# Projecting layer 0 of a graph network by 22 tiles of 128 rows while its neighbour sums stay in 24 blocks of 113

## The chip, the cores and the metric

The kernel runs on one core of a Trainium2 chip. The metric is device microseconds of one execution of the whole program, the median of several runs. The engines are called PE (TensorE, matmuls), DVE (VectorE), ACT (ScalarE), POOL (GpSimd) and SP (SyncE, which here only issues DMAs). Each runs its own instructions in order.

## The reference

Four layers share one sparse adjacency matrix of 2708 x 2708 (about five entries in a row) and node features of 2708 x 512, all float32. After each layer the features are added to the layer's result and normalized over their 512 columns. Only layer 0 and what layer 1 reads from it matter here:

```python
# layer 0
e1 = adj @ x
e2 = e1 * (learnable_diag_1 + 1.0)
x1 = layernorm(x + (x - e2) @ weight + bias)
# what layer 1 reads of x1
h  = x1 @ W_sa                      # 512 columns, and two score columns h @ a_sa
hb = x1 @ W_gcnb                    # 512 columns
# and four gate columns x1 @ Wa, x1 @ Wb (two halves of each)
```

Layer 1 then sums h with attention weights and hb with the adjacency's values over neighbours; layers 2 and 3 aggregate over the same neighbours.

## The kernel before

The adjacency is used as lists. Its rows are cut into 24 blocks of R = 113 rows (`rows(i)`, the last has 109), so that one block's entries fit into 4 chunks of 128. For each block the kernel loads the 113 columns of the transposed adjacency (`load_adj`, three buffers in turn), finds the nonzero entries on DVE, brings them into a list, fetches the neighbours' rows of x from HBM with 4 indirect DMAs on POOL (`gather`), and sums them on PE with a spread matrix as the stationary operand.

The order on every engine is written out by hand, in a prologue and then a loop over `k` from 1 to 23. In step k different blocks are at different stages:

- Block k+3 is searched. `find` runs over four segments of the block's columns, a `max` and a `max_index` each (L831, L833); `count` (from L845) then computes where each entry goes. `negatives` is a 2.3 us pass of ACT over the block, `clear_diagonal` one of POOL.
- Block k+2 becomes a list. `starts` is a tiny matmul (L873), `ranges` its two ACT operations (`middle`, L880, and `q`, L881) and one on DVE (`rec_all`, L882), `mark` a comparison on DVE (L890), `fetch` four matmuls (L895) that need the mark, `pick` ten small DVE operations (L904 to L933) that need the fetch and start the gather, `values0` eight ACT operations that make the spread matrix.
- Block k+1 is summed: `sums0` (l0a on PE, L611), `inputs0` on DVE (L958 to L964: own rows times the diagonal entry, plus sum, times the diagonal weights, plus own rows; the last of the four adds the bias to the own rows `xi` for later), and `turn_u` (tr_l: four transposes on PE and a copy by ACT).
- Block k is projected: `project0` (o_l on PE, L582), `residual0` (L975 on DVE, then ACT), `norm0` (ACT writes the new features to `xr[:, k, :]` in SBUF).
- Block k-1 gets its part of layer 1's table: `turn_x` (tr_x), `next0` (h on PE in two halves of 259 columns, the last six of which are scores and gates and are copied to `cols[:, i, :]`), `rest0` (hb on PE), and `store0` one step later, which sends the rows to `table[0]` in HBM.

The order within a step is what the prediction walks through. On PE it is starts, tr_x, o_l, fetch, h, l0a, hb, tr_l of the next block. On DVE it is rec_all, one search, mark, one search, residual, pick, two searches, count, inputs. `move_rows` splits a row move so that its first part has a multiple of 16 rows. After the loop, layer 1 begins with gathers from `table[0]`, which need every row of it.

Of the kernel before, what the change touches and what calls it, by code (L numbers as in the profile page):

```python
# [12 lines left out]
P = 128  # L13
# [5 lines left out]
R = 113  # L19
# [428 lines left out]
def sparse_stack(  # L448
# [51 lines left out]
    xr = big.tile([P, NB, D], FP, name="xr")  # L500
# [48 lines left out]
    cols = const.tile([P, NB, 6], FP, name="cols")  # L549
# [13 lines left out]
    def move_rows(r, dst, src):  # L563

        c = r // 16 * 16
        for a, b in ((0, c), (c, r)):
            nc.sync.dma_start(out=dst(a, b), in_=src(a, b))

    def turned(u, r, name):

        tr = ps_tr.tile([P, DB, P], FP, tag="tr", name=f"tr_{name}")
        for f in range(DB):
            nc.tensor.transpose(tr[:, f, :r], u[:r, f * P : (f + 1) * P], ident[:r, :r])  # L573
        uT = work.tile([P, DB, P], FP, tag="uT", name=f"uT_{name}", bufs=3)
        nc.scalar.copy(uT[:, :, :r], tr[:, :, :r])  # L575
        return uT
# [65 lines left out]
    with ExitStack() as phase:  # L642
# [41 lines left out]
        def load_own(i):  # L684
            r = rows(i)
            xi = work.tile([P, D], FP, tag="xi", name=f"xi{i}", bufs=3)
# [6 lines left out]
        )  # L693
        gath0 = [
            gflat[k // 2][:, k % 2 * EC * D :][:, : EC * D].rearrange("p (c d) -> p c d", d=D)
            for k in range(4)
        ]
        nc.scalar.memzero(gflat[0])
# [90 lines left out]
        def turn_w(k):  # L789
# [3 lines left out]
            wT = work.tile([P, DB, P], FP, tag="uT", name=f"w_saT{k}", bufs=3)  # L793
# [81 lines left out]
        def ranges(i):  # L875

            t = made[i]
            q = lst.tile([P, EC * P], FP, tag="q", name=f"q{i}")
# [21 lines left out]
        def pick(i):  # L900
# [28 lines left out]
            gather(gath0[i % 4], i, x, D)  # L929
# [21 lines left out]
        def sums0(i):  # L951
            agg0[i] = aggregate(spread0.pop(i), gath0[i % 4], rows(i), f"l0a{i}")

        def inputs0(i):
# [9 lines left out]
            nc.vector.tensor_add(xi[:r, :], xi[:r, :], b0_bc[:r, :])  # L964
            u0[i] = u

        def project0(i):
            o0[i] = project(turned0.pop(i), rows(i), w0_sb, f"l0_{i}")

        def residual0(i):  # L970

            r = rows(i)
            v = work.tile([P, D], FP, tag="v", name=f"l0v{i}")
            stats = small.tile([P, 5], FP, tag="stats0", name=f"st_l0_{i}")
            nc.vector.scalar_tensor_tensor(  # L975
                v[:r, :], o0.pop(i)[:r, :], 0.0, own.pop(i)[:r, :], op0=ALU.add, op1=ALU.add,
# [10 lines left out]
            v0[i] = v, stats  # L987

        def norm0(i):
            r = rows(i)  # L990
            v, stats = v0.pop(i)
# [3 lines left out]
                xr[:r, i, :], v[:r, :], AF.Identity, bias=stats[:r, 4:5], scale=stats[:r, 3:4]  # L995
            )

        def next0(i):

            r = rows(i)  # L1000
            xT = turned0["x", i]
            st = st_ring[i % 2]
            half = (D + 6) // 2
            ends = (0, half, D)
            for k in range(2):
                o = ps_o.tile([P, D], FP, tag="o", name=f"h{k}_{i}")
# [5 lines left out]
            nc.scalar.copy(cols[:r, i, :], col)  # L1012
            nc.scalar.copy(st[:r, 2 * D + 1 : 2 * D + 4], col[:, 1:4])
            st0[i] = st

        def rest0(i, between=lambda: None):
            xT = turned0.pop(("x", i))
            o = ps_o.tile([P, D], FP, tag="o", name=f"hb_{i}")
            times(o[: rows(i), :], xT, rows(i), w_gc_sb, between)
            st0[i] = st0[i], o  # L1020

        def store0(i):
            r = rows(i)
            st, o = st0.pop(i)
            nc.scalar.copy(st[:r, D + 1 : 2 * D + 1], o[:r, :])
            move_rows(
                r, lambda a, b: table[0][i * R + a : i * R + b, :], lambda a, b: st[a:b, :]
            )

        def turn_u(i):  # L1030
            turned0[i] = turned(u0.pop(i), rows(i), f"l0_{i}")

        def turn_x(i):
            turned0["x", i] = turned(xr[:, i, :], rows(i), f"x1_{i}")
# [94 lines left out]

        project0(0)  # L1130
        find(3, (0,), places=False)
        starts(2)
        ranges(2)
        gate_columns()
        turn_w(0)
        mark(2)
        fetch(2)
        find(3, (0,), values=False)
        residual0(0)
        turn_w(1)  # L1140
        pick(2)
        own[2] = load_own(2)
        sums0(1)
        times_a(0)
        turn_w(2)
        norm0(0)
        inputs0(1)
        times_a(1)
        turn_w(3)
        turn_u(1)  # L1150
        values0(2)
        times_a(2)
        times_a(3)
        score_rows()
        find(3, (1, 2, 3))
        clear_diagonal(4)
        count(3)
        negatives(3)
        load_adj(6)
# [6 lines left out]
        for k in range(1, NB):  # L1166
            m, b = k + 2, k + 3
            if k == 1:
                turn_x(k - 1)
                project0(k)  # L1170
            if m < NB:
                starts(m)
                if k == 1:
                    score_columns()
                ranges(m)
            if k > 1:
                turn_x(k - 1)
                project0(k)
                store0(k - 2)
            if b < NB:  # L1180
                negatives(b)
                find(b, (0,))
            if m < NB:
                mark(m)
                if k > 1:
                    fetch(m)
            if b < NB:
                find(b, (1,))
            residual0(k)
            if b + 1 < NB:  # L1190
                clear_diagonal(b + 1)
            if k == 1:
                next0(k - 1)
                fetch(m)
            if m < NB:
                pick(m)
                own[m] = load_own(m)
            norm0(k)
            if k > 1:
                next0(k - 1)  # L1200
            if m < NB:
                values0(m)
            if b < NB:
                find(b, (2, 3))
# [581 lines left out]
```

## Time and profile before

| | |
|---|---|
| median of 3 runs | 1010.57 us (1010.06 to 1011.61) |
| profiled execution | 996.16 us, of which the span is 994.3 us |
| PE, DVE, ACT, POOL busy in the span | 92%, 71%, 53%, 48% |
| mean granted PE clock | 0.97 |
| one step of the loop in its steady part | 15.95 us |
| last matmul of layer 0 (hb of block 23) ends | 427.8 us into the span |
| first gather of layer 1 | 432.95 us |
| DMA share, 100 to 375 us | 0.38 to 0.75 |

The engines' busy times overlap. PE's busy time is a model of pipelined matmuls; the distance from one group's start to the next's is the better measure of what a group takes, and the prediction uses that. A float32 matmul over 4 slices of 128 shows as 8 records.

### The profile page before, as it was taken

The page shows a single profiled execution, that of the slowest core. Times are in us where ns is not written, and L with a number is a line of the kernel's source. Part 1 is how long each engine was busy: PE and PEld are TensorE (multiplying, and loading weights), DVE is VectorE, ACT ScalarE, POOL GpSimd, SP SyncE. Part 2 cuts the span into 40 slices and gives each one's busy share as a digit, 9 for nine tenths or more (in the row PEclk, how much of TensorE's full clock was granted, in tenths as well). Part 3 has the DMA queues.
Part 4 walks back from the last instruction along what each step waited for, and adds up shares of the span by engine and source line. Part 5 has one row for each costly group of instructions (what it writes and reads, how often), then busy time and mean ns, then how long its engine had stood idle before and what let it go on. Part 6 is the DMA issues. An engine that isn't in the chain of part 4 may idle for free. (4 is left out here: it accounts for less than half of the span.)

```text
span 994.3 us, 11251 instructions
## 1 busy us (share of the span) xinstructions
PE 913.7 (92%) x3037; PEld 496.8 (50%) x3037; DVE 709.1 (71%) x1956; ACT 528.3 (53%) x1174; POOL 480.1 (48%) x543
## 2 busy tenths in 40 slices
PE   7889999999999999988888888889988989999994
PEld 3445555555555555546666666633333334444441
DVE  7788888888888883238888878858777615555543
ACT  5676676766667674346767767415455412322222
POOL 3232323323132322045666666467777568776640
PEclk8899999999999999989999999979999999999998
DMA  9965757575665533368999999346777656555531
GB/s 248 286 157 163 198 154 204 160 205 162 191 185 160 152 106 104 94 200 271 315 304 306 312 301 295 122 142 201 219 210 228 176 149 180 169 169 162 167 109 31
DMA packets 126715, 190.55 MB, mean 192 GB/s; under 512 B 81065, under 2 KB 81111, under 8 KB 126643
## 3 DMA queue, kind: packets, MB, share of 16 engines
q0 software_dynamic: 36864, 111.73, 38.4%
q1 hardware_dynamic: 89779, 78.02, 27.5%
q8 instruction: 26, 0.43, 0.2%
q14 instruction: 46, 0.38, 0.1%
HBM read 176.28 MB, written 27.80 MB: 205 GB/s over the span
## 5 line engine op out<-in xcount | busy, mean ns | idle before, releaser
L598 POOL DMA_INDIRECT gath<-table,source x288 | 314.9, 1093 | 139.7 <-issue 66.7
L598 POOL DMA_INDIRECT gath<-in_x_dram,source x96 | 96.7, 1007 | 261.3 <-issue 222.7
L1347 PE MATMUL l1s<-gath,s 128*113 128x256 f32 (+3 forms) x384 | 94.6, 401 | 26.8 <-DVE l1b L1377 26.6
L611 PE MATMUL l2a<-gath,s_left 128*113 128x512 f32 (+1 forms) x192 | 96.5, 623 | 13.0 <-DMA gath<-table,source 10.2
L575 ACT COPY uT_l<-tr_l 128x452 f32<-128x452 f32 (+1 forms) x48 | 25.9, 540 | 138.2 <-PE tr_l L573 138.2
L1347 PEld LDWEIGHTS l1s<-gath,s 128*113 128x113 f32 (+1 forms) x384 | 68.9, 184 | 52.9 <-DVE l1b L1377 34.8
L582 PE MATMUL o_l<-w_sb,uT_l 128*113 128x512 f32 (+1 forms) x192 | 91.8, 623 | 2.2 <-ACT uT_l L575 1.1
L611 PE MATMUL l3a<-gath,s 128*113 128x512 f32 (+1 forms) x192 | 88.5, 603 | 3.5 <-DMA gath<-table,source 3.5
L582 PE MATMUL h<-w_sa_sb,uT_x 128*113 128x259 f32 (+1 forms) x384 | 88.3, 382 | 0.8 <-ACT w_sa_sb L815 0.8
L1357 PE MATMUL l1e<-gath,e 128*113 128x257 f32 (+3 forms) x384 | 87.1, 379 | 0.4 <-DVE e L1340 0.4
L582 PE MATMUL o_l<-shared,uT_l 128*113 128x512 f32 (+1 forms) x192 | 86.5, 593 | 0.6 <-ACT uT_l L575 0.6
L611 PE MATMUL l0a<-gath,s 128*113 128x512 f32 (+1 forms) x192 | 87.1, 596 | 0.0
L582 PE MATMUL hb<-w_gc_sb,uT_x 128*113 128x512 f32 (+1 forms) x192 | 86.6, 593 | 0.0
L1357 PEld LDWEIGHTS l1e<-gath,e 128*113 128x113 f32 (+1 forms) x384 | 68.0, 177 | 15.9 <-DVE e L1340 0.8
L582 PEld LDWEIGHTS h<-w_sa_sb,uT_x 128*113 128x113 f32 (+1 forms) x384 | 66.1, 177 | 16.1 <-issue 1.0
L1705 ACT ACTIVATE y<-l3v,mv_l 113x512 f32<-113x512 f32 (+1 forms) x24 | 19.5, 813 | 88.0 <-DVE mv_l L1701 83.5
L611 PEld LDWEIGHTS l2a<-gath,s_left 128*113 128x113 f32 (+1 forms) x192 | 30.6, 182 | 68.6 <-DMA gath<-table,source 40.7
L582 PEld LDWEIGHTS o_l<-shared,uT_l 128*113 128x113 f32 (+1 forms) x192 | 33.9, 178 | 48.8 <-issue 47.0
L582 PEld LDWEIGHTS hb<-w_gc_sb,uT_x 128*113 128x113 f32 (+1 forms) x192 | 33.9, 178 | 46.5 <-issue 41.5
L582 PEld LDWEIGHTS o_l<-w_sb,uT_l 128*113 128x113 f32 (+1 forms) x192 | 33.2, 183 | 45.6 <-issue 38.5
L611 PEld LDWEIGHTS l3a<-gath,s 128*113 128x113 f32 (+1 forms) x192 | 32.4, 180 | 42.3 <-issue 39.1
L611 PEld LDWEIGHTS l0a<-gath,s 128*113 128x113 f32 (+1 forms) x192 | 34.2, 179 | 38.4 <-issue 36.7
(244 smaller groups left out, 1644.8 us busy)
## 6 DMA issues: line engine op xcount, KB each, us to landing
shared<-in_adj_dram SPq DMA_DIRECT2D x14, 1186.5 KB
table<-st SPq DMA_DIRECT2D x23, 450.2 KB
shared<-table SPq DMA_DIRECT2D x23, 448.0 KB
gath<-in_adj_dram SPq DMA_DIRECT2D x7, 1186.5 KB
xi<-in_x_dram SPq DMA_DIRECT2D x23, 224.0 KB
table<-xr SPq DMA_DIRECT2D x23, 224.0 KB
table<-y SPq DMA_DIRECT2D x23, 224.0 KB
out_dram<-y SPq DMA_DIRECT2D x23, 224.0 KB
```

Source lines behind the costliest of these rows:

```text
L575: nc.scalar.copy(uT[:, :, :r], tr[:, :, :r])
L582: nc.tensor.matmul(o, lhsT=uT[:, f, :r], rhs=w[:, f, :], start=(f == 0), stop=(f == DB - 1))
L598: nc.gpsimd.indirect_dma_start(out=g[:, c, :n], out_offset=None, in_=src[:, :], in_offset=bass.IndirectOffsetOnAxis(ap=source[:, i, c : c ...
L611: nc.tensor.matmul(agg[:r, :], lhsT=s[:, c, :r], rhs=g[:, c, off : off + D], start=(c == 0), stop=(c == EC - 1),)
L1347: nc.tensor.matmul(sum_s[i][:r, k, : at.stop - at.start], lhsT=s[:, c, :r], rhs=g[:, c, at], start=(c == 0), stop=(c == EC - 1),)
L1357: nc.tensor.matmul(sum_e[i][:r, k, k : k + at.stop - at.start], lhsT=e[:, c, :r], rhs=g[:, c, at], start=(c == 0), stop=(c == EC - 1),)
L1705: nc.scalar.activation(y[:r, :], v[:r, :], AF.Identity, bias=mv[:r, 3:4], scale=mv[:r, 2:3])
```

## The change

The sums, lists and searches stay in blocks of 113 rows. The projections, the norm, and layer 1's table are now computed by 22 windows of 128 rows (the last has 20). `turn_u` still transposes a block at a time, but ACT copies its columns into the one or two windows that they belong to (`uw`, three buffers). A window is projected in the first step in which all its rows are there, one window a step at most: `window_at` maps steps to windows, and steps 8 and 17 have none. Its own rows of x are loaded once more (`load_window`), and `bias0` adds the bias to those. The new features are written to `x1w`, in window order, and `to_blocks` moves them and the six score and gate columns by DMA to the block order of `xr`, whose rows become 518 wide and hold `cols` at their end.

The search is taken out of the steps: `search(n)` does the next n segments wherever they belong. A step does four; in steps 3, 4, 5, 12, 13, 14 it does five, in steps 9 and 18 (after a step without a window) one. Projection 0 moves from the prologue into the loop, which now has 26 steps, from 0. The windows' buffers take half of a gather buffer, so there are three gather buffers for four, and two of `uT` and `xi` for three. `load_diagonal` and two tiny loads move ahead of the loop.

```diff
-    xr = big.tile([P, NB, D], FP, name="xr")
+    xr_cols = big.tile([P, NB, D + 6], FP, name="xr")
+    xr = xr_cols[:, :, :D]
...
+        def load_window(w):
+            move_rows(
+                wrows(w), lambda a, b: xw[w % 2][a:b, :],
+                lambda a, b: x[w * P + a : w * P + b, :],
+            )
+
+        def to_blocks(w):
+
+            g, end = w * P, w * P + wrows(w)
+            while g < end:
+                i, q = g // R, g % R
+                n = min(end, (i + 1) * R) - g
+                move_rows(
+                    n, lambda a, b: xr_cols[q + a : q + b, i, :],
+                    lambda a, b: x1w[w % 2][g - w * P + a : g - w * P + b, :],
+                )
+                g += n
...
-            nc.vector.tensor_add(xi[:r, :], xi[:r, :], b0_bc[:r, :])
+            own.pop(i)
             u0[i] = u
+        def bias0(w):
+            r = wrows(w)
+            nc.vector.tensor_add(xw[w % 2][:r, :], xw[w % 2][:r, :], b0_bc[:r, :])
...
         def turn_u(i):
-            turned0[i] = turned(u0.pop(i), rows(i), f"l0_{i}")
+            u, r = u0.pop(i), rows(i)
+            tr = ps_tr.tile([P, DB, P], FP, tag="tr", name=f"tr_l0_{i}")
+            for f in range(DB):
+                nc.tensor.transpose(tr[:, f, :r], u[:r, f * P : (f + 1) * P], ident[:r, :r])
+            a = i * R
+            while a < i * R + r:
+                w = a // P
+                b = min(i * R + r, (w + 1) * P)
...
+                nc.scalar.copy(
+                    window_uT[w][:, :, a - w * P : b - w * P], tr[:, :, a - i * R : b - i * R]
+                )
+                a = b
...
+        window_at, step = {}, 0
+        for w in range(KB):
+            step = max(step + 1, (min(w * P + P, N) - 1) // R)
+            window_at[step] = w
+        to_find = [(b, g) for b in range(3, NB) for g in range(NG)]
+        def search(n):
+            for _ in range(min(n, len(to_find))):
+                b, g = to_find.pop(0)
+                if g == 0:
+                    negatives(b)
+                find(b, (g,))
+                if g == 1 and b + 1 < NB:
+                    clear_diagonal(b + 1)
+                if g == NG - 1:
+                    count(b)
+                    if b + NA < NB:
+                        load_adj(b + NA)
...
+        for k in range(NB + 2):
+            m = k + 2
+            w, wx = window_at.get(k), window_at.get(k - 1)
+            parts = 4
+            if any(t not in window_at for t in (k + 3, k + 4, k + 5)) and 2 < k < NB - 6:
+                parts = 5
+            if k > 2 and wx is None:
+                parts = 1
             if m < NB:
                 starts(m)
...
                 ranges(m)
+            if wx is not None and k <= NB:
+                turn_x(wx)
+            if w is not None:
+                project0(w)
+            if k - 2 in window_at:
+                store0(window_at[k - 2])
+            search(1)
             if m < NB:
                 mark(m)
+                fetch(m)
...
+            if parts > 1:
+                search(1)
+            if w is not None:
+                residual0(w)
             if m < NB:
                 pick(m)
                 own[m] = load_own(m)
+            if k + 1 in window_at:
+                load_window(window_at[k + 1])
+            if w is not None:
+                norm0(w)
+            if wx is not None:
+                next0(wx)
             if m < NB:
                 values0(m)
+            search(parts - 2)
             if k + 1 < NB:
                 sums0(k + 1)
                 inputs0(k + 1)
+            if k + 1 in window_at:
+                bias0(window_at[k + 1])
...
+            if wx is not None:
+                rest0(wx, (lambda: turn_x(w)) if k == NB else (lambda: None))
             if k + 1 < NB:
                 turn_u(k + 1)
...
```

## The prediction

> **What bounds the kernel now.** I first read the table of 25 us windows: for each, the busy time of TensorE (PE), its weight loads, VectorE (DVE), ScalarE (ACT) and GpSimd (POOL), then PE's granted clock, the DMA share and GB/s.
>
> ```profile
> core 0: us, PE busy (x) PEld busy (x) DVE busy (x) ACT busy (x) POOL busy (x), PEclk, DMA share, GB/s
> 50.00:75.00 25.00, 21.84 (x84) 11.51 (x83) 21.85 (x64) 19.58 (x45) 7.31 (x9) 0.98 0.65 157
> 250.00:275.00 25.00, 24.89 (x99) 14.86 (x98) 21.53 (x64) 17.75 (x40) 5.68 (x6) 1.00 0.61 172
> 400.00:425.00 25.00, 24.77 (x89) 13.76 (x89) 6.57 (x20) 7.84 (x26) 0.00 (x0) 1.00 0.25 70
> ```
>
> From about 72 us to 428 us, the end of layer 0, PE never rests, DVE has about a seventh of its time free, DMA a third. Before 72 us PE does wait. The chain of waits only covers layer 3, which is untouched, so layer 0 has to be read from PE's timeline. One steady step (start, duration, instructions; in brackets an idle time before it and what ended it):
>
> ```profile
> 249.58 0.55 PE L573 MATMUL tr_l<-ident,l0u 113*128 113x113 f32 x4
> 249.97 0.29 PE L873 MATMUL fetched<-totals,under 128*128 128x1 f32 x2
> 250.12 0.58 PE L573 MATMUL tr_x<-ident,xr 113*128 113x113 f32 x4
> 250.76 3.69 PE L582 MATMUL o_l<-w_sb,uT_l 128*113 128x512 f32 x8
> 254.29 1.03 PE L895 MATMUL fetched<-rec_all,q 128*128 128x96 f32 x8
> 255.15 3.68 PE L582 MATMUL h<-w_sa_sb,uT_x 128*113 128x259 f32 x16
> ```
>
> After it come l0a (258.66) and hb, each 3.43 long, and the next tr_l at 265.53: a step is 15.95 us. Start to start, o_l takes 3.53, the fetch 0.86, h 3.51. The same step on DVE:
>
> ```profile
> 246.34 0.75 DVE L958 SCALAR_TENSOR_TENSOR l0u<-xi,adiag,l0a 113x512 f32<-113x512 f32 x1 [0.32 <-PE l0a L611]
> 247.85 0.69 DVE L963 TENSOR_TENSOR l0u<-l0u,xi 113x512 f32<-113x512 f32 x1
> ...
> 250.80 0.19 DVE L882 SCALAR_TENSOR_TENSOR rec_all<-fetched,far 128x32 f32<-128x32 f32 x1 [1.53 <-ACT middle L880]
> 252.65 0.47 DVE L890 TENSOR_SCALAR q<-q,totals 128x512 f32<-128x512 f32 x1
> ```
>
> DVE's first work of a step, rec_all, starts 1.22 us after tr_l and its last that PE needs, L963, ends at 248.6, 1.0 us before tr_l. With the 0.32 us wait for l0a, **DVE's slack is only 1.3 us a step**. The mark (L890) releases PE's fetch, with 1.2 us to spare now.
>
> Last, what PE's idle times cost:
>
> ```profile
> 72.37 0.58 PE L573 MATMUL tr_l<-ident,l0u 113*128 113x113 f32 x4 [2.27 <-DVE l0u L963]
> ...
> 73.58 5.39 PE L582 MATMUL o_l<-w_sb,uT_l 128*113 128x512 f32 x8
> ...
> 452.28 5.43 PE L1347 MATMUL l1s<-gath,s 128*113 128x256 f32 x16 [3.01 <-DVE l1b L1377]
> 484.88 3.74 PE L1347 MATMUL l1s<-gath,s 128*113 128x256 f32 x16 [1.95 <-DVE l1b L1377]
> 577.99 5.43 PE L1347 MATMUL l1s<-gath,s 128*113 128x256 f32 x16 [1.93 <-DVE l1b L1377]
> ```
>
> Idles of 1.93, 2.27 and 3.01 us were followed by half clock and 1.7 us lost; one of 1.95 was not.
>
> **What the Trainium skill says.** "TensorE: Matmul & The Clock Gate", section "Back-to-back issue gap", has the spacing depend on the columns streamed, not on the rows kept. The trace agrees: hb of the last block, 109 rows, takes 3.43 us as with 113. Section "What's actually happening" gates the clock after an idle window of about 3.4 us; here idles near 2 us already did it in part of the cases, so I use the trace. Section "Step-by-step: what each phase is for" says matmuls stay in program order, only weight loads move ahead: so a fetch that waits holds h behind it. "DMA: Bandwidth & Descriptors", "Issuing engines are not separate DMA queues": all queues share 16 engines; the added moves must fit into the 0.61 share.
>
> **The change, part by part** (reference 996.2 us, the profiled execution, of which the span is 994.3; the runs' median is 1010.57, 1.4% more, so I add the difference to that).
>
> *Two projections fewer.* 22 windows for 24 blocks removes two each of o_l, h and hb, some 21 us of PE in all. Where they go decides. In step k, o_l is of window w and h, hb of the window of step k-1. A window needs the block holding its last row, so w stands at step (128w+127)//113: 1 to 7, not 8, then 9 to 16, not 17, 18 to 23; the last, of 20 rows, at 24. Counted from step 2 (72.37 us), the new loop drops o_l in steps 8 and 17 and tr_x, h, hb in 9 and 18, but adds step 24 and moves everything one step later. Net: one o_l, h, hb and tr_x: 3.53 + 3.51 + 3.43 + 0.39 = **-10.9 us**. The other set leaves the head.
>
> *Head.* Until 72.37 DVE ends last (tr_l waited 2.27 us for it). It loses block 0's residual (0.75), one 0.69 us add that now follows the inputs, and about 2 us of waits: for ACT's middle behind the 2.3 us negatives (1.59 at 58.7 us) and for PE's o_l of block 0. It keeps all 8 searches and the wait for the Sqrt chain. The window load that bias0 waits for is queued behind two adjacency blocks, which stop loading DMA at 46 us, and the diagonal loads (4.0 us of SP): landed by about 52, needed at 53. I take **-3.3** (bounds -5 to 0, as PE will be cold there).
>
> *Full steps.* 17 stay. turn_u now copies in two pieces. A 452-element ACT copy takes 0.54, one of 6 elements 0.17, so about 0.17 fixed: both pieces 0.70. o_l needs only the first, so it starts some 0.1 us earlier: **-1.7**; middle and rec_all come 0.18 later, within DVE's slack. A transpose of 128 rows adds 0.05, counted. Other edits cost nothing: the bias add moved behind the inputs that PE waits for; two uT, two xi and three gather buffers suffice, since each is last read a step before it is refilled; a gather is issued over 5.2 us, from 8 us into a step, and read 15 us later.
>
> *Five searches in steps 3, 4, 5, 12, 13, 14* (one in 9 and 18). A search is 1.5 to 1.75 us of DVE; 1.0 of slack at L963, less than 0.1 at l0a after the 0.18: tr_l is late by about 0.65. Six times: **+3.9**. Afterwards each list's last search and count() (1.3 us) stand ahead of mark, in steps 6 to 9 and 15 to 18. Fetch comes 0.15 late in the full ones: **+0.6**.
>
> *The gap steps.* In step 8 there is no o_l to cover mark. From tr_l: rec_all 1.22, search from 1.33 to 2.83, count and hand-over 1.31, mark 0.47, so fetch at 4.65; PE is idle from 0.97, **3.7 us, as long as the o_l it dropped**. Then fetch 0.86, h 3.51, l0a 3.43, hb 3.43: 15.9, the old step again. Step 9: mark ends at 4.7, fetch until 5.6, l0a until 9.05; no hb covers DVE's three input operations (2.3), so tr_l waits 2.4: 11.5. Step 10's first copy is 0.2 late behind values0. Together 27.6 where 2 x 15.95 - 0.2 - 10.9 = 20.8 would be free of waits: +6.75, twice: **+13.5**.
>
> *Clock.* Idles of 3.7 us in steps 8 and 17: 1.7 each; those of 2.4 before 10 and 19, half of the time: **+5.1** (0 to 8).
>
> *Moves.* Per window SP gains one load of 256 KB and up to four SBUF copies (265 KB), each priced near the 0.3 us that a row move takes now: under 2 us of SP's 16, where it is about 5 busy. Their bytes are about 2 us of DMA at the 310 GB/s of the step's full stretches, while some 3.5 us of a step are idle. norm0 waits for the copies of two steps earlier. No later work is queued behind them but the next adjacency load, two steps early. I take 0, up to +10, if window loads land after bias0 and hold DVE; none below zero, as they only add work.
>
> *End of layer 0.* Layer 1's first gather waits for the last table rows: ACT copy done at 428.6, gather at 432.95. 20 rows instead of 109: **-1.1** (0 to -2). cols now arrive by DMA, a price the trace lacks for SBUF to SBUF; at about 3 us as for that table store they land before the exp table is loaded (429.9). xr's wider row changes no element count: 0.
>
> Sum: -10.9 - 3.3 - 1.7 + 3.9 + 0.6 + 13.5 + 5.1 - 1.1 = **+6.1 us**: 1002.3 profiled, 1016.7 as median.
>
> **Rivals.** (1) *The cover works*: 21 us of PE really vanish, if ACT and DVE enter a gap step ahead of PE. For it: DVE has 14% free and the three searches done early shorten step 9. Against: rec_all hangs on tr_l, which PE itself issues, so DVE can't be ahead. With gap losses of 4 instead of 13.5 and no cold clock: -8.5, 1002 us; it decides where the two pairs lose less than about 12 us in all, clock included. (2) *They cancel*: the clock stays up and the head gains 5: about -0.7, 1009.9. (3) *DMA or SP becomes the bound*: window load behind an adjacency load in steps 6, 7, 15, 16, where that now comes early: +6 on top, 1023. (4) The change not doing what it says: 22 PE groups are in its instruction order, so no.
>
> **Numbers.** My forecast 0.58, rival 1 0.16, rival 2 0.12, rival 3 0.14. 0.2%, 2 us, is about what can be told from no change. Faster 0.16, same 0.12, slower 0.72. The range, 1004 to 1025, leaves out most of rival 1 and takes in a clock loss of 8 and part of the moves' bound.
>
> **What would show it.** Steps of 15.85 us; 16.5 where five searches run; PE idle of about 3.7 us ahead of fetch in steps 8 and 17 with h slow behind it, and 2.4 us ahead of tr_l a step later; hb of the last window ending near 435 us, from 427.8; layers 1 to 3 as long as now. Gap pairs of 21 to 23 us would prove me wrong, and so would DVE waiting for a DMA at bias0.

## The result and the profile after

| | before | after | ratio, 95% interval |
|---|---|---|---|
| median, first comparison | 1010.06 us (5 runs) | 1019.53 us (1016.02 to 1020.60, 5 runs) | 1.0089 (1.0067 to 1.0110) |
| median, second comparison | 1009.23 us | 1020.61 us | 1.0138 (1.0104 to 1.0171) |
| layer 0 ends in the profile (last hb) | 427.8 us | 437.8 us; 440.3 in a second profile | |
| span of the profiled execution | 994.3 us | 1016.9 us; 1014.7 | |

The change makes the kernel slower by 0.9% to 1.4%, 9.5 us in the first comparison, where 6.1 was forecast. The profiled spans lie 22.6 us apart. Of this 10.0 are layer 0; the other 12.6 are not the change's, as the first experiment shows. Each set of runs below came from one chip, and the time after layer 0 goes with the chip and not with the kernel: 565 to 567 us in the four profiles from chip 4 and in the first profile of the kernel before, 574 to 583 in the eight from chips 2, 13 and 15 and in the first profile after (on which chips the two first profiles ran is not known). The medians differ in the same way (the kernel before has 993 us on chip 4, 1009 to 1012 on the others), so only ratios within one set are compared. Layer 0's end is read as the start of the matmul that follows the last hb.

First the table of 25 us windows of the changed kernel, with the columns as before: the span's stretch, its length, busy times of PE, PEld, DVE, ACT and POOL, then PE's granted clock, DMA share and GB/s.

```profile
core 0: us, PE busy (x) PEld busy (x) DVE busy (x) ACT busy (x) POOL busy (x), PEclk, DMA share, GB/s
50.00:75.00 25.00, 19.74 (x67) 9.48 (x66) 20.48 (x60) 16.07 (x34) 7.59 (x9) 0.90 0.82 219
250.00:275.00 25.00, 24.52 (x92) 14.96 (x92) 23.11 (x74) 14.43 (x36) 4.62 (x6) 1.00 0.82 225
400.00:425.00 25.00, 24.89 (x81) 12.70 (x80) 7.54 (x21) 7.84 (x25) 0.00 (x0) 1.00 0.46 139
```

In the middle line, a stretch with five searches in a step, DVE is now busy 23.1 of 25 us, from 21.5, and the DMA share is 0.82, from 0.61: little of DVE's slack is left there. PE still works 24.5 of the 25 us.

PE's timeline of the changed kernel shows where it rests. A step is counted from one tr_l to the next. In order: the start of step 2, the start of step 5 behind a five-search step, steps 8 and 9 and the start of 10, a steady step (11), and the start of step 19.

```profile
70.71 0.99 PE L1071 MATMUL tr_l<-ident,l0u 113*128 113x113 f32 x4 [4.99 <-DVE l0u L991]
...
122.79 0.58 PE L1071 MATMUL tr_l<-ident,l0u 113*128 113x113 f32 x4 [0.50 <-DVE l0u L991]
...
171.35 0.55 PE L1071 MATMUL tr_l<-ident,l0u 113*128 113x113 f32 x4
...
176.03 2.02 PE L923 MATMUL fetched<-rec_all,q 128*128 128x96 f32 x8 [3.50 <-DVE q L918]
177.85 4.48 PE L584 MATMUL h<-w_sa_sb,uT_x 128*128 128x259 f32 x16
182.16 3.60 PE L613 MATMUL l0a<-gath,s 128*113 128x512 f32 x8
185.60 3.60 PE L584 MATMUL hb<-w_gc_sb,uT_x 128*128 128x512 f32 x8
189.03 0.55 PE L1071 MATMUL tr_l<-ident,l0u 113*128 113x113 f32 x4
...
200.74 0.58 PE L1071 MATMUL tr_l<-ident,l0u 113*128 113x113 f32 x4 [2.39 <-DVE l0u L991]
...
216.56 0.55 PE L1071 MATMUL tr_l<-ident,l0u 113*128 113x113 f32 x4
...
217.57 3.61 PE L584 MATMUL o_l<-w_sb,uw 128*128 128x512 f32 x8
...
343.21 0.94 PE L1071 MATMUL tr_l<-ident,l0u 113*128 113x113 f32 x4 [2.38 <-DVE l0u L991]
```

Step 8 runs from 171.35 to 189.03, 17.68 us: the fetch waits 3.50 us for the mark (L918), takes 2.02 us where 1.03 is its usual time, and h 4.48 for 3.69: half clock through the fetch and into h. Step 9 is 11.71 us long and ends in 2.39 us of idle. The steady step ends at 232.28, so it is 15.72 us. tr_l in step 19 takes 0.94 us, half clock again after an idle of 2.38; the same idle ahead of step 10 left the clock up (0.58).

DVE's timeline in step 8 gives the reason for the 3.50 us. The lines are the first work of the step, its first search (two lines), and the mark; left out are the search's load line and the nine operations of `count`.

```profile
172.57 0.19 DVE L910 SCALAR_TENSOR_TENSOR rec_all<-fetched,far 128x32 f32<-128x32 f32 x1 [2.25 <-ACT middle L908]
172.68 0.74 DVE L859 MAX8 rec_all<-shared 128x8 f32<-128x565 f32 x1
...
173.53 0.74 DVE L861 FIND_INDEX8 where_all<-rec_all,shared 128x8 uint32<-128x565 f32 x1
...
175.50 0.48 DVE L918 TENSOR_SCALAR q<-q,totals 128x512 f32<-128x512 f32 x1
```

DVE waits 2.25 us for ACT's middle, which hangs on tr_l of PE; then 1.5 us of search and 1.3 us of count go ahead of the mark, and with no o_l on PE nothing runs beside them.

### The profile page after: what moved, and what is told of

Its sections match the earlier page's. It is cut to its first block, busy times and chain, and to the rows that moved or that the text cites. A ratio compares the mean times of both kernels' runs of the same rounds, so it can differ in the third digit from the quotient of the medians.

```text
span 1016.9 us, 11285 instructions
## 1 busy us (share of the span) xinstructions
PE 905.9 (89%) x2965; PEld 502.1 (49%) x2965; DVE 703.7 (69%) x1948; ACT 522.0 (51%) x1171; POOL 475.2 (47%) x543
## 4 chain that ended last, share of the span: by engine, by line
PE 59%; DVE 19%; DMA 8%; issue 5%; POOL 3%; ACT 2%; another core or an unknown queue 2%; SPq 0%; POOLq 0%; DVEq 0%; ACTq 0%
PE o_l L584 12%; PE l2a L613 9%; PE l3a L613 8%; DMA gath<-table,source 7%; PE l0a L613 6%; PE h L584 6%; PE hb L584 5%; PE unread L1523 4%; DVE where_all L861 3%; DVE rec_all L859 3%; POOL gath L600 2%; PE fetched L923 2%; PE tr_l L1071 1%; PE tr_l L575 1%
## 5 line engine op out<-in xcount | busy, mean ns | idle before, releaser
L613 PE MATMUL l2a<-gath,s_left 128*113 128x512 f32 (+1 forms) x192 | 94.1, 634 | 2.1 <-DVE s_left L1560 2.0
L613 PE MATMUL l0a<-gath,s 128*113 128x512 f32 (+1 forms) x192 | 89.9, 613 | 0.0
L584 PE MATMUL o_l<-w_sb,uw 128*128 128x512 f32 (+1 forms) x176 | 83.5, 618 | 0.7 <-ACT uw L1080 0.4
L584 PE MATMUL h<-w_sa_sb,uT_x 128*128 128x259 f32 (+1 forms) x352 | 83.6, 391 | 0.0
L584 PE MATMUL hb<-w_gc_sb,uT_x 128*128 128x512 f32 (+1 forms) x176 | 79.5, 593 | 0.0
L584 PEld LDWEIGHTS h<-w_sa_sb,uT_x 128*128 128x128 f32 (+1 forms) x352 | 65.5, 191 | 12.8 <-issue 1.8
L1523 PE MATMUL unread<-bg_bc,ident 128*128 128x512 f32 x88 | 47.6, 662 | 20.6 <-remote 16.3
L613 PEld LDWEIGHTS l2a<-gath,s_left 128*113 128x113 f32 (+1 forms) x192 | 34.9, 192 | 52.5 <-issue 47.1
L1732 DVE SCALAR_TENSOR_TENSOR l3v<-o_l,d_inv,b_bc 113x512 f32<-113x512 f32 (+1 forms) x25 | 18.1, 729 | 55.4 <-PE o_l L584 50.5
L584 PEld LDWEIGHTS hb<-w_gc_sb,uT_x 128*128 128x128 f32 (+1 forms) x176 | 32.5, 186 | 40.9 <-issue 39.5
```

The costliest lines, as they stand in the source:

```text
L584: nc.tensor.matmul(o, lhsT=uT[:, f, :r], rhs=w[:, f, :], start=(f == 0), stop=(f == DB - 1))
L613: nc.tensor.matmul(agg[:r, :], lhsT=s[:, c, :r], rhs=g[:, c, off : off + D], start=(c == 0), stop=(c == EC - 1),)
L1523: nc.tensor.matmul(o[:, :cols], lhsT=ident, rhs=bg_bc[:, :cols], start=True, stop=True)
L1732: nc.vector.scalar_tensor_tensor(v[:r, at], o[:r, at], d_inv[:r, i : i + 1], b3_bc[:r, at], op0=ALU.mult, op1=ALU.add,)
```

## The experiments

All runs below are profiled. Layer 0's end is a sharp measure: the unchanged kernel ends it at 427.8 and at 427.9 us, with steps of 15.95 both times, and it goes along with the measured ratio. In the changed kernel the chance of the clock moves it by 2.5 us (437.8 and 440.3), so differences of that size between two rows say little by themselves; the lengths of the steps say more.

| kernel | layer 0 ends, us | against 427.8 | ratio to the kernel before, 95% interval |
|---|---|---|---|
| before, again | 427.9 | +0.1 | 1.0009 (0.9990 to 1.0027) |
| after, again | 440.3 | +12.5 | 1.0138 (1.0104 to 1.0171) |
| h ahead of the fetch, moves too | 441.4 | +13.6 | 1.0144 (1.0108 to 1.0179) |
| mark ahead of the search | 432.9 | +5.1 | 1.0036 (1.0018 to 1.0055) |
| fillers in the idle times | 433.1 | +5.3 | 1.0063 (1.0037 to 1.0089) |
| h ahead, moves left in place | 431.3 | +3.5 | 1.0043 (1.0025 to 1.0061) |
| four searches in every step | 440.9 | +13.1 | 1.0125 (1.0095 to 1.0155) |
| moves twice | 442.0 | +14.2 | 1.0151 (1.0105 to 1.0196) |
| bias add on POOL | 445.9 | +18.1 | 1.0156 (1.0125 to 1.0186) |
| starts a step early | 434.1 | +6.3 | 1.0055 (1.0028 to 1.0082) |
| all together | 424.8 | -3.0 | 0.9979 (0.9953 to 1.0004) |
| all together, second form | 427.8 | 0.0 | 0.9976 (0.9947 to 1.0004) |

### The kernel before, a second time

No edit.

> The kernel before, unchanged, profiled a second time. In the two profiles the part after layer 0 lasts 566.5 us before the change (994.3 - 427.8) and 579.1 us after it (1016.9 - 437.8), although its code is the same. Theory A, executions of one program differ by that much in layers 1 to 3: layer 0 again ends at 427.8 within 0.5 us, and the rest takes about 579, a span near 1007 to 1009, which is what the median of 1010 asks for. Theory B, the change itself slows the later layers (other addresses, other instruction positions): again 427.8 and 566.5, a span near 994.

Measured: layer 0 ends at 427.9; the span is 1006.3 us, so the rest lasts 578.4. The line below is from PE's waits after 640 us (in total, times, longest); "remote" is a wait whose end the profile can't place on this core.

```profile
PE unread L1470 <- remote: 18.2, 4, 7.1
```

The first profile of the changed kernel has four such waits too, in the same code of layer 2:

```profile
PE unread L1523 <- remote: 16.3, 4, 5.9
```

The first profile of the kernel before has none. Theory A holds in that the kernel does not matter: 12 us between the two first profiles were a difference of executions. Over all profiles, two to four such waits are there in each one from chips 2, 13 and 15 and none in the four from chip 4. What they are stays open.

### Fillers in the idle times

```diff
                 mark(m)
+                if k in (8, 17):
+                    keep_busy(4)
                 fetch(m)
...
                 inputs0(k + 1)
+                if k in (9, 18):
+                    keep_busy(2)
```

> Unread matmuls fill PE's idle times: four of 128x512 (0.86 us each, 3.4 in all) ahead of fetch in steps 8 and 17, two ahead of tr_l at the end of steps 9 and 18. They do no useful work and free no wait; they only keep PE running. Clock theory: fetch and h of steps 8 and 17 run at full clock, 17.7 becomes 15.9 twice, and step 19 (17.40) becomes 15.75: the last hb ends at 432.6 instead of 437.8, -5.2. Rival, the slow h and fetch are not due to the idle time: 437.8, or later by what the fillers stand in the way.

Measured: 433.1 us. PE's timeline of step 8:

```profile
172.48 3.60 PE L798 MATMUL unread<-gath,ident 128*128 128x512 f32 x8
176.15 1.13 PE L923 MATMUL fetched<-rec_all,q 128*128 128x96 f32 x8
177.12 3.69 PE L584 MATMUL h<-w_sa_sb,uT_x 128*128 128x259 f32 x16
```

The fetch starts as late as before, but it and h run at full clock: the step takes 16.04 us for 17.68, step 17 16.03 for 17.72, step 19 15.95 for 17.40. So the clock cost 4.7 us in steps 8, 17 and 19 of the first profile of the changed kernel. It is not a fixed price: in the second profile of that kernel the same step reads as follows.

```profile
175.53 2.02 PE L923 MATMUL fetched<-rec_all,q 128*128 128x96 f32 x8 [3.50 <-DVE q L918]
177.34 5.91 PE L584 MATMUL h<-w_sa_sb,uT_x 128*128 128x259 f32 x16
```

The idle is the same 3.50 us, but h takes 5.91 us, the step 19.11, and step 10 was at half clock as well (17.42). Against the run with fillers steps 8, 10, 17 and 19 lose 7.7 us there. The Trainium skill, "TensorE: Matmul & The Clock Gate", section "What's actually happening", has the clock decided by a free-running window of about 3.4 us; one such window at half clock costs 1.7 us and two cost 3.4 (an estimate from that page). The losses fit, 1.4 to 1.7 us at most places and 3.1 at this one, and so does a free-running window, as equal idles of 2.4 us ended both ways. That the clock falls only after an idle window does not fit: 2.4 us were enough.

### The changed kernel, a second time

No edit.

> The changed kernel, unchanged, profiled a second time beside the others. If layer 0 is as repeatable as in the kernel before (427.9 and 428.0), its last hb ends at 437.8 within 2 us, where the 2 us are the step after an idle time of 2.4 us, which ran at half clock in one of two cases; total about 9 us over the kernel before on the same chip.

Measured: 440.3 us, 2.5 more than the first profile. Steps 8 and 10 are together 3.0 us longer, all of it clock, step 2 is 0.5 shorter; every other step is within 0.05 us of the first profile. The expected 2 us were a little exceeded, since one idle cost 3.1 us of clock and not 1.6.

### Mark ahead of the search in the steps without o_l

```diff
-            search(1)
+            late = w is None and m < NB
+            if not late:
+                search(1)
             if m < NB:
                 mark(m)
                 fetch(m)
+            if late:
+                search(1)
```

> In steps 8 and 17 only, mark and fetch go ahead of the search with its count. The bytes and the instructions are the same, only 2.8 us of DVE work move behind mark. Theory A, cover alone: fetch starts 1.9 us after tr_l instead of 4.7, the idle falls from 3.50 to about 1.0 us, no cold clock: 0.97 + 1.0 + 0.86 + 3.51 + 3.43 + 3.43 = 13.2 instead of 17.7. Theory B, DVE next: the same sum of DVE work as in the run with h first, so also about 14.0, and the last hb again ends near 428.8. Theory C, the mark is not what fetch waits for: 437.8.

PE in step 8 and at the start of step 9:

```profile
173.30 1.13 PE L923 MATMUL fetched<-rec_all,q 128*128 128x96 f32 x8 [1.33 <-DVE q L918]
174.27 3.69 PE L584 MATMUL h<-w_sa_sb,uT_x 128*128 128x259 f32 x16
...
185.43 0.58 PE L1071 MATMUL tr_l<-ident,l0u 113*128 113x113 f32 x4 [0.61 <-DVE l0u L991]
```

The idle falls from 3.50 to 1.33 us and the clock stays up, so the mark was what the fetch waited for. But the step takes 14.65 us, not the 13.2 of theory A: tr_l now waits 0.61 us for DVE. Theory B holds, at 0.65 us more than worked out. The end, 432.9, is later than its 428.8 by those 0.65 us twice and because steps 10 and 19 both ran at half clock (17.53 and 17.40).

### h ahead of the fetch

```diff
+            gap = w is None and m < NB
+            if gap and wx is not None:
+                next0(wx)
             search(1)
...
-            if wx is not None:
+            if wx is not None and not gap:
                 next0(wx)
```

> In the steps without o_l (8 and 17) h of the previous window is put ahead of the fetch on PE. Theory A, the missing cover alone makes the gap: fetch no longer waits for mark, h runs at full clock, step 8 takes 0.97 + about 0.7 for the uT_x copy + 3.51 + 0.86 + 3.43 + 3.43 = 12.9 us instead of 17.68, twice, and step 19 is no longer cold (-1.65): the last hb ends at 426.6 instead of 437.8. Theory B, DVE is the next bound: its 12.7 us of work from rec_all to the end of l0u, begun 1.25 us after tr_l, put the next tr_l at 14.0 us: -3.7 twice and -1.65, 428.8. Theory C, the idle is not the cover's but comes from elsewhere (a transfer, the DVE chain as a whole): no change, 437.8.

Measured: 441.4 us, worse than the changed kernel. Step 8 takes 14.86 us, near theory B's 14.0, but step 9 takes 18.39 for 11.71. The three views, SP's queue, DVE and PE, in this order:

```profile
176.77 2.77 SPq L569 DMA_DIRECT2D xr<-gath  x4
179.66 0.41 SPq L669 DMA_DIRECT2D shared<-in_adj_dram  x1
180.12 2.68 SPq L673 DMA_DIRECT2D shared<-in_adj_dram  x1
182.85 0.66 SPq L569 DMA_DIRECT2D xi<-in_x_dram  x2
183.55 0.35 SPq L569 DMA_DIRECT2D gath<-in_x_dram  x1
```

```profile
190.67 0.69 DVE L997 TENSOR_TENSOR gath<-gath,gath 128x512 f32<-128x512 f32 x1 [5.92 <-DMA gath<-in_x_dram]
191.28 0.18 DVE L910 SCALAR_TENSOR_TENSOR rec_all<-fetched,far 128x32 f32<-128x32 f32 x1
```

```profile
194.73 2.02 PE L923 MATMUL fetched<-rec_all,q 128*128 128x96 f32 x8 [5.28 <-DVE q L918]
```

`next0` also issues the moves of the finished rows (xr<-gath). Put early, they wait on SP for h's copy until 176.77 and hold the adjacency load, and behind it the window load, which goes out at 183.55, 7.1 us before DVE's bias add (L997) can use it. DVE works in order, so rec_all, the mark and PE's fetch stand behind that add. None of the three theories had this; it is rival 3 of the prediction, made by the experiment itself.

### h ahead of the fetch, the moves left in their place

```diff
             st0[w] = st
-            to_blocks(w)
...
             if wx is not None and not gap:
                 next0(wx)
+            if wx is not None:
+                to_blocks(wx)
```

> As the run with h first, but the moves of finished rows to their blocks (and with them SP's issues) stay where the change has them, behind the window load; only the matmuls of h and their copies go ahead of the fetch. In the run with h first, bias0 of step 9 waited 5.92 us for the window load, and mark and the fetch behind it 5.28. Theory A, that wait is SP's order: the moves waited for h's copy at 176.7 and held the adjacency load and the window load behind them (issued 183.55): steps 9 and 18 return from 18.4 and 13.9 to about 11.7, the last hb from 441.4 to 432.5. Theory B, h ahead of the fetch is itself what delays DVE and the fetch: it stays near 441.

Measured: 431.3 us; steps 9 and 18 take 11.73 us. Theory A holds: SP's order alone had cost 6.7 and 2.2 us. PE in step 8, and at the start of step 9:

```profile
174.51 3.76 PE L584 MATMUL h<-w_sa_sb,uT_x 128*128 128x259 f32 x16 [1.29 <-ACT uT_x L577]
...
186.90 0.58 PE L1070 MATMUL tr_l<-ident,l0u 113*128 113x113 f32 x4 [0.88 <-DVE l0u L991]
```

Step 8 takes 14.85 us and ends with PE waiting for DVE, as it did with the mark put first. Two different edits meet the same bound: a step without o_l has nearly as much DVE work as any other, and it begins only when tr_l has led to middle and rec_all. It is a bound of this order and not of the work: with the mark put first and the early starts together, in a later run, the step takes 12.35 us. That steps 10 and 19 kept their clock here (15.82 and 15.85) is chance.

### Moves issued twice

```diff
             to_blocks(w)
+            to_blocks(w)
```

> Every move of finished rows into blocks is issued twice, the second time with the same bytes: SP issues 2.8 us more per window, and the DMA engines carry another 0.26 MB. The forecast priced the moves at nothing: then the last hb stays at 437.8 and steps at 15.75 and 16.46. Rival, SP's queue and the DMA order are at their limit: the next adjacency load and window load come 2.8 us later, bias0 waits for its load as it did for 5.92 us in the run with h first, mark and fetch behind it, and steps 9 and 18 or the full ones grow: 442 or more.

Measured: 442.0 us, 4.2 more. DVE and PE in step 6:

```profile
141.15 0.69 DVE L997 TENSOR_TENSOR gath<-gath,gath 128x512 f32<-128x512 f32 x1 [3.11 <-DMA gath<-in_x_dram]
```

```profile
145.21 1.13 PE L923 MATMUL fetched<-rec_all,q 128*128 128x96 f32 x8 [2.20 <-DVE q L918]
146.18 5.37 PE L584 MATMUL h<-w_sa_sb,uT_x 128*128 128x259 f32 x16
```

Step 6 grows from 16.12 to 20.07 us, idle and cold clock. Its like nine steps on, step 15, grows by only 0.1, and what the clock's chances add in steps 8 and 10 they take off in 2 and 19. Over the run DVE's bias add waits 13.0 us in six places for a window load, in the first profile of the changed kernel 2.4 us in three, the longest 1.30 in step 10, which still takes only 15.82. So the forecast's price of nothing was nearly right for the moves as they are, but the margin is less than one more set of them.

### Four searches in every step

```diff
-                parts = 5
-            if k > 2 and wx is None:
-                parts = 1
+                parts = 4
```

> Four searches in every step, none with five, none with one. By the prediction's sizes as the profile after has them: six five-search steps give back 0.65 each (-3.9), the four steps 6, 7, 15, 16 their 0.35 (-1.4), steps 8 and 17 the 1.3 us of count() ahead of mark (-2.6); against that steps 9 and 18 carry three more searches, 5.0 us of DVE, where DVE has about 1.8 to spare: 11.7 becomes 14.9, +6.4. Last hb 436.3 instead of 437.8. Rival: if the five-search steps are slow for another reason than the search (the moves, the window load), they stay at 16.46 and the last hb goes to about 441.

Measured: 440.9 us, near the rival's number but not for its reason. Steps 3 to 5 go to 15.75 to 15.85, so the search does make the five-search steps long. Steps 9 and 18 grow to 14.83 and 14.85, as worked out. Steps 8 and 17, at 16.63 and 16.61, gain 1.1 each where 1.3 was expected. What was left out is the clock: PE's idle at the end of step 9 is now 5.99 us, and steps 10 and 19 take 17.43 and 18.83.

```profile
200.88 0.99 PE L1071 MATMUL tr_l<-ident,l0u 113*128 113x113 f32 x4 [5.99 <-DVE l0u L991]
```

So four searches everywhere bring nothing: the end lies beside the 437.8 and 440.3 of the change, and which of the two is better is not shown.

### The bias add on POOL

```diff
-            nc.vector.tensor_add(xw[w % 2][:r, :], xw[w % 2][:r, :], b0_bc[:r, :])
+            nc.gpsimd.tensor_add(xw[w % 2][:r, :], xw[w % 2][:r, :], b0_bc[:r, :])
```

> The bias add of each window (0.69 us on DVE, at the end of a step) goes to POOL, which is busy 91 of 367 us there. Theory A, DVE's load is what makes the five-search steps long and puts its searches behind a window load: 16.46 becomes 15.8 six times, 16.1 becomes about 15.8 four times: -5.1, the last hb at 432.7; steps 8 and 17 keep their idle of 3.5 us, since that hangs on mark. Theory B, PE's own work or ACT sets these steps: no change, 437.8. Theory C, POOL holds its gathers behind the wait for a window load or slows DVE by as much: 438 or later.

Measured: 445.9 us. Steps 3 and 4 stay at 16.50 and 16.48, since on DVE the add had stood in time that DVE spends waiting: ahead of rec_all of step 4 it now waits 1.45 us for ACT's middle, in the changed kernel 0.85. And where POOL's add falls beside DVE's work, it holds it. POOL, then DVE, in step 5:

```profile
138.32 1.09 POOL L997 TENSOR_TENSOR gath<-gath,gath 128x512 f32<-128x512 f32 x1
```

```profile
138.14 1.83 DVE L990 TENSOR_TENSOR l0u<-l0u,gath 113x512 f32<-113x512 f32 x1
140.00 0.69 DVE L991 TENSOR_TENSOR l0u<-l0u,xi 113x512 f32<-113x512 f32 x1
```

L990 takes 0.69 to 0.79 us in the changed kernel and 1.83 here, 1.04 more, while POOL's add takes 1.09. The Trainium skill, "SBUF — State Buffer", section "SBUF: two separate sides", says that a GpSimd operation and a VectorE operation with two SBUF inputs exclude each other, and that the one that starts first keeps the other out for its whole instruction. The trace agrees on the first: in seven steps L990 takes 1.71 to 2.05 us and ends 0.56 us after POOL's add, while the searches (0.86) and the first input operation (L986, 0.73 to 0.75, one input from PSUM) keep their time beside it. It does not show the second, as L990's record begins 0.05 to 0.39 us ahead of POOL's, whose times are rough. Theory C holds, at a price of 8.1 us against the first profile of the changed kernel and 5.6 against the second; some 3 us of it are in steps 5, 11, 14, 20 and 21, and most of the rest is clock (step 8 took 18.95).

### Starts and ranges a step early

```diff
-            if m < NB:
+            if k < 3:
                 starts(m)
                 if k == 2:
                     score_columns()
                 ranges(m)
...
                 inputs0(k + 1)
+            if 1 < k and m + 1 < NB:
+                starts(m + 1)
+                ranges(m + 1)
```

> From step 2 on, starts and ranges of the next list (PE's middle, ACT's copy and Abs, DVE's rec_all) are issued at the end of a step, between l0a and hb, and no longer behind tr_l of the next step. With the bias add on POOL the five-search steps stayed at 16.5, so it is not DVE's sum of work that makes them long, but the chain tr_l, middle, rec_all, five searches, l0u. Theory A, that chain: rec_all no longer hangs on tr_l, DVE goes on at once (0.85 to 1.7 us a step): 16.46 becomes 15.8 six times (-3.9), steps 6, 7, 15, 16 15.8 (-1.3), mark of steps 8 and 17 comes about 1.7 us earlier, their idle 3.5 becomes 1.8 (-1.7 twice): the last hb 429.2 instead of 437.8. Theory B, the five searches are too many for DVE whatever it waits for: 16.46 stays and only steps 8 and 17 gain, 434.

Measured: 434.1 us. Steps 8 and 17 take 13.75 us for 17.7: the fetch waits 1.17 us. The five-search steps take 16.15, 16.46 and 16.10 us, so they gain 0.3 at most. DVE's waits from 70 to 440 us (in total, times, longest), first in the changed kernel:

```profile
DVE rec_all L910 <- ACT middle L908: 25.7, 18, 2.2
DVE l0v L1007 <- PE o_l L584: 20.2, 6, 7.3
```

and with the early starts:

```profile
DVE l0v L1007 <- PE o_l L584: 37.4, 17, 8.0
...
DVE rec_all L910 <- ACT middle L908: 3.2, 4, 1.6
```

22.5 us of waits at rec_all are gone, and 17.2 are back one place later, at the residual, which needs PE's o_l. Neither theory is right as it stands, though the end is theory B's: the early wait goes, but in a full step DVE's chain then begins at o_l, as the two waits suggest. Steps 8 and 17 gain more than twice what was expected. Steps 10 and 19 got longer (19.80 and 18.66): there ACT's copy for o_l now stands behind values0 and middle, and the clock went down.

### All together

The early starts, the mark ahead of the search in steps 8 and 17, and fillers ahead of tr_l:

```diff
                 score_rows()
+                keep_busy(5)
...
+            if k in (9, 18):
+                keep_busy(2)
```

> All that the runs point to, together: starts and ranges at the end of the step before; in steps 8 and 17 mark and fetch ahead of the search; unread matmuls in PE's idle times ahead of tr_l of step 2 (five) and of steps 10 and 19 (two each). By theory A of the run with starts moved alone: 16.46 to 15.8 six times (-3.9), four times -0.3 (-1.3), steps 8 and 17 from 17.7 to 13.6 (DVE's 13.4 us of work, -4.1 twice), step 19 warm (-1.5), step 2 warm (-2.5): the last hb near 420.4, 7.4 us ahead of the kernel before (427.9), which is 0.7% of the whole. If theory B holds there: about 425. If fillers or the early starts delay PE: 430 or more.

Measured: 424.8 us, 3.0 ahead of the kernel before and 13 of the changed one; ratio 0.9979 (0.9953 to 1.0004). Steps 8 and 17 take 12.35 us, step 2 16.65 for 19.14. In step 8 PE has no wait left. Five-search steps stay at 16.1 to 16.5 as in the run before, steps 10 and 19 at 16.95, some 5 us in all; steps 6, 7, 15 and 16 and the head lose 2 more against the expected 420.4, and steps 8 and 17 win back 2.5 (12.35 for 13.6). Its ratio lies below both of the changed kernel, intervals included. Against the kernel before, the gain in the profile is there and the timed interval just includes none.

A second form left starts of steps 10 and 19 in place and moved a search into steps 9 and 18:

```diff
-                parts = 1
+                parts = 2
...
-            if 1 < k and m + 1 < NB:
+            if 1 < k and m + 1 < NB and wx is not None:
```

> As the run with all of it together, whose layer 0 ended at 424.8, with two edits. Starts and ranges stay at the start of steps 10 and 19, where ACT's copy for o_l had stood behind values0 and the middle (o_l waited 0.9 us, step 16.95): back to about 15.9, -1.0 twice. Steps 9 and 18, which have 1.15 us of DVE idle and little work, take two searches instead of one, so one five-search step of each three is left out (16.46 to 15.95, -0.5 twice). Theory, these are the places where layer 0 still loses: the last hb ends at 421.8, 6.1 us ahead of the kernel before, 0.6% of the whole. Rival, DVE is at its limit in steps 9 and 18 too and tr_l of the next step comes later by a search: 424.8 or more.

Measured: 427.8 us, as the rival had it. PE at the start of step 19:

```profile
331.31 0.60 PE L1071 MATMUL tr_l<-ident,l0u 113*128 113x113 f32 x4 [1.28 <-DVE l0u L991]
...
333.71 5.40 PE L584 MATMUL o_l<-w_sb,uw 128*128 128x512 f32 x8 [1.17 <-ACT uw L1080]
```

tr_l waits 1.28 us for DVE behind the fillers, o_l another 1.17 for its copy, and step 19 takes 19.11 us at a mean clock of 0.91. Leaving out one five-search step gained nothing: step 4 fell from 16.46 to 16.04 us and step 5 rose from 16.09 to 16.49. The half clock of o_l is 1.7 us of the distance to the first form, and the two timed ratios, 0.9976 and 0.9979, don't tell the forms apart.

## Why the prediction was nearly right

| layer 0, against the kernel before, us | forecast | first profile | second profile |
|---|---|---|---|
| start of step 2 (head) | -3.3 | -1.7 | -1.7 |
| step 2 | -0.1 | +1.5 | +0.9 |
| six five-search steps | +3.3 | +2.9 | +2.9 |
| steps 6, 7, 15, 16 | +0.2 | +0.6 | +0.6 |
| steps 8, 9, 17, 18 with the clock they cost | +18.6 | +18.9 | +21.9 |
| two projections fewer and the other steps | -11.5 | -12.2 | -12.2 |
| end of layer 0 | +7.2 | +10.0 | +12.5 |

The fifth row counts from the 20.8 us that the prediction gave for a pair of gap steps free of waits, and takes in what steps 10 and 19 are over 15.75.

- *Two projections fewer, -10.9, and o_l earlier, -1.7.* Right: full steps take 15.72 to 15.82 us, from 15.95, and the row of the table, which is what the other rows leave of the whole, is 0.7 beyond its forecast. ACT's two pieces take 0.60 us together and not 0.70, so o_l starts 1.01 us after tr_l, from 1.18.
- *The gap steps.* Right in place, cause and size. The fetch waits 3.50 us for 3.7, tr_l 2.39 for 2.4, and the pair with the clock kept up by fillers takes 16.04 + 11.61 = 27.65 us for 15.9 + 11.5 = 27.4. The runs with the mark or with h put first show that the idle was the mark's, and that DVE's chain of one step, from rec_all on, stands right behind it.
- *Clock, +5.1.* 4.7 measured with fillers, by chance as many half-clock places as assumed; 7.7 in the second profile. The range of 0 to 8 was the honest statement.
- *Five searches.* 16.46, 16.48 and 16.34 us for 16.5. The forecast called it DVE's slack; the runs with the bias on POOL and the early starts show a chain: work taken out of DVE's waits brings nothing, and the waits move to the next thing that PE owes.
- *Head, -3.3.* This is the term that was mis-sized: -1.7. The residual and the order of the add did go (1.4 us). The "about 2 us of waits" did not: DVE's waits from 43.8 us to the end of the head were 2.9 us before and 2.5 after. In place of ACT's middle behind the negatives there is 0.37 for the fetch and 0.83 for the middle, 0.47 us for the first window load, landed at 54.8 and not by 52, and 0.57 for the Sqrt chain. In the second profile the load landed at 55.7, and DVE waited 2.52 us for it. The waits in question, before, after and in the second profile:

```profile
58.69 0.19 DVE L882 SCALAR_TENSOR_TENSOR rec_all<-fetched,far 128x32 f32<-128x32 f32 x1 [1.59 <-ACT middle L880]
```

```profile
54.80 0.69 DVE L997 TENSOR_TENSOR gath<-gath,gath 128x512 f32<-128x512 f32 x1 [0.47 <-DMA gath<-in_x_dram]
```

```profile
55.73 0.69 DVE L997 TENSOR_TENSOR gath<-gath,gath 128x512 f32<-128x512 f32 x1 [2.52 <-DMA gath<-in_x_dram]
```

The head's other cost stood in the prediction's bound ("as PE will be cold there") and not in its sum: with no projection in the head, PE's clock is 0.64 from 25 to 50 us (0.84 before), and PE idles 4.99 us ahead of step 2, which takes 19.14 us (18.63 in the second profile) where the old one, cold as well, took 17.68. The run with five fillers there brought it to 16.65.

- *Moves at nothing.* Nearly right. The sign that was to prove the forecast wrong, DVE waiting for a DMA at bias0, did appear: 2.4 us in the first profile, 3.4 in the second, but outside the head no step shows more than about 0.1 us for it. The moves did not fit into the DMA share of 0.61 but came on top of it (0.82). The bound of +10 was earned: issued twice they cost 4 us in one step, and in the run with h first a window load issued 13.5 us into step 8, for 8.6 in the changed kernel, and its like in step 17 cost 9.
- *End of layer 0, -1.1.* The first gather of layer 1 comes 3.65 us after the last hb, for 5.18 before, so -1.5. But layer 1's first sums start 13.5 us after it, for 11.7. PE stops for 2.32 us ahead of bias_rows with nothing that the profile shows to wait for, in both profiles of the changed kernel and in neither of the kernel before. The edits of the changed kernel that ran on chips 13 and 15 all show it (1.9 to 2.5 us); the four that ran on chip 4, and the second form of all together, don't. Its cause is open; POOL and PE at that place:

```profile
441.46 1.00 POOL L600 DMA_INDIRECT gath<-table,source  x1 [51.62 <-DMA table<-st]
```

```profile
449.32 2.04 PE L1497 MATMUL bias_rows<-bg_bc,one_row 1*128 1x512 f32 x2 [2.32 <-issue]
```

- *Rivals.* The cover working and the cancelling are excluded: the two pairs take 29.39 and 29.42 us, so they lose 17.2 by their waits and clock, above the 12 from which rival 1 was to decide. Rival 3 is not in the change but close beside it: steps 6, 7, 15 and 16 lost 0.6 us in all. Adding the difference to the runs' median and not to the profiled span was right: layers 1 to 3 of the first profile belong to an execution that ran them 12 us faster.

The change cost 9.5 us for 6.1, so the forecast is 3.4 short, about what the first two rows are off by, 3.2; the other rows nearly cancel.

## What to carry to other kernels

Work taken off one engine is worth time only where the other engines lose work in the same step: here PE lost o_l in two steps, DVE kept all of its own work there but 1.4 us (the residual and one add), and the dropped matmuls came back as idle time, with a colder clock on top. When an operation is dropped, ask what it covered; when a wait is removed, look one place further along the same engine, and move an instruction only together with a look at every queue on which it issues, DMAs included.

## What was not expected of the hardware

- Equal idles of PE cost unequal time: 3.50 us was followed by a loss of 1.6 us in one execution and 3.1 in another, 2.4 us by none or by 1.4 to 1.7.
- An add on POOL of 1.09 us lengthened a DVE operation with two SBUF inputs from 0.79 to 1.83 us; in seven steps it ended 0.56 us after the add did.
- Layers 1 to 3, unchanged, took 565 to 567 us in five of the fourteen profiles, among them all four from chip 4, and 574 to 583 in the others; layer 0 of the kernel before took the same to 0.2 us in both kinds.
